# Scratch matrix products around the group-norm chains of a four-layer block

## The chip, the cores and the metric

One core of one Trainium2 chip runs the whole program. The metric is the device time of one execution in microseconds (us). A kernel is executed several times and the median is given; beside it stands one execution that the hardware profiler recorded.

## The reference, cut to what matters

The input is one image of 256 x 256 positions with 128 channels, in 32-bit floats. Four layers follow each other, and each adds its result to its own input after a group norm over the whole image:

```python
def _gn(v, G=32, eps=1e-5):
    g = v.reshape(B_, H_, W_, G, C_ // G)
    m = jnp.mean(g, axis=(1, 2, 4), keepdims=True)
    s = jnp.var(g, axis=(1, 2, 4), keepdims=True)
    return ((g - m) / jnp.sqrt(s + eps)).reshape(v.shape)

x = x + _L0_conv_ref(_gn(x), ...)   # attention along the rows, 4 heads
x = x + _L1_conv_ref(_gn(x), ...)   # a gated recurrence of 16 steps
x = x + _L2_conv_ref(_gn(x), ...)   # products over pairs of rows, gated
x = x + _L3_conv_ref(_gn(x), ...)   # a 3x3 convolution and a 128x128 matrix
```

A group is 4 neighbouring channels over all positions. So no layer can apply its norm before the last element of the layer in front of it is there: the mean and the variance of the whole image stand between any two layers.

## The kernel before, in words

Channels lie on the 128 partitions, positions along the free dimension. Each layer streams the image from DRAM in blocks, computes, writes its sum back to DRAM and gathers statistics as it goes. The four stages are the methods `attention`, `recurrence`, `triangle` and `convolution`; `run` (L1475) calls them in that order.

**The group norm between stages.** `group_affine` (L75) turns the statistics of 128 channels into a scale and an offset for each channel, the two columns of the tile `ab`. It is a chain of tiny steps that wait for each other:

1. VectorE makes mean and variance of each channel, `mv` (L99 to L120; in the first stage they come from `statistics`).
2. TensorE averages the means over a group: `pm`, a product with the 128x128 matrix `g4` and one moving column (L81).
3. VectorE copies it to `mg`, and forms the group's variance terms `gd` and `gv` (L83 to L87).
4. TensorE averages those: `pv` (L89).
5. ScalarE takes the root, `sd` (L91); VectorE makes `ab` from it (L93, L94).

Every product goes through the helper `mm` (L59, its line in the profile is L60). In float32 one product is recorded as two TensorE instructions, "passes" below, and two weight loads. `group_affine` is called four times:

- L352, in `attention`, after `statistics`. After it come `centering` (L129: the tile `lc` and the product `pc`), and then the block loop: transposes `pt` (L394), their copies `xo` (L395), the centring products `zc` (L403), their copies `zs` (L405), and so on.
- L845, in `recurrence`. After it come the products `pab` (L852) and `rpbf`, `rpbi`, `rpbd` (L860) with `ab`, and the block loop, whose first products are the gate `zd` (L912), then `za`, `m`, `zf`.
- L1075, in `triangle`. After it come `centering`, a product `tpbo` (L1081) and the block loop with `zc` (L1137), `zs` (L1139).
- L1365, in `convolution`. After it the taps `U` get a term (L1369), a bias tile `bw` is made through the product `cpbw` (L1374, L1375), ScalarE normalises rows into `xp` (L1394), VectorE transforms them into `v` (L1411 to L1426), and TensorE multiplies `v` with `U` into `m` (L1436): 24 x 3 products of 128x128 for each half block of 8 rows, 32 half blocks. VectorE and ScalarE turn `m` into output rows (L1444 to L1458), POOL issues their store (L1460).

**What sets the order.** A scheduler arranges the instructions of each engine by its own estimate of their times, except those that were given to `keep_in_program_order` (`pin`), which stay in the order of the code. Each engine works its list in order and waits there on semaphores. Tiles come from pools: a new tile takes the place of an older one, and its first writer waits for the last reader of the old one. PSUM pools are opened and closed around each stage, so the small pools around `group_affine` (`awq` L351, `rwp` L844, `twp` L1074, `cxp` L1364) take banks that the stage before has just used.

Of the kernel before, what the change touches and what calls it, by code (L numbers as in the profile page):

```python
# [9 lines left out]
F32 = mybir.dt.float32  # L10
# [7 lines left out]
P = 128  # L18
# [12 lines left out]
class Kernel:  # L31
# [27 lines left out]
    def mm(self, out, lhsT, rhs, start=True, stop=True):  # L59
        return self.nc.tensor.matmul(out, lhsT, rhs, start=start, stop=stop)  # L60

    def column(self, pool, src, name):

        t = pool.tile([src.shape[0], 1], F32, name=name)
        self.nc.sync.dma_start(t, src.rearrange("(c o) -> c o", o=1))
        return t
# [5 lines left out]

    def group_affine(self, pool, psum, stats, group, tag, whole=False, shift=None, mv=None):  # L75

        nc = self.nc
        if mv is None:
            mv = self.mean_variance(pool, stats, tag, shift)
        pm = psum.tile([P, 2], F32, name=f"pm{tag}", tag="gn")  # L80
        self.mm(pm[:, 0:1], group, mv[:, 0:1])  # L81
        mg = pool.tile([P, 1], F32, name=f"mg{tag}")
        nc.vector.tensor_copy(mg, pm[:, 0:1])  # L83
        d = pool.tile([P, 1], F32, name=f"gd{tag}")
        nc.vector.tensor_sub(d, mv[:, 0:1], mg)
        v = pool.tile([P, 1], F32, name=f"gv{tag}")
        nc.vector.scalar_tensor_tensor(v, d, d, mv[:, 1:2], ALU.mult, ALU.add)  # L87
        pv = psum.tile([P, 2], F32, name=f"pv{tag}", tag="gn")
        self.mm(pv[:, 0:1], group, v)  # L89
        sd = pool.tile([P, 1], F32, name=f"sd{tag}")  # L90
        self.chain("table", self.act(sd, pv[:, 0:1], AF.Sqrt, bias=self.eps))  # L91
        ab = pool.tile([P, 2], F32, name=f"ab{tag}")
        nc.vector.reciprocal(ab[:, 0:1], sd)  # L93
        nc.vector.scalar_tensor_tensor(ab[:, 1:2], mg, -1.0, ab[:, 0:1], ALU.mult, ALU.mult)  # L94
        if whole:
            return ab, mg, sd
        return ab
# [961 lines left out]
    def triangle(self, x2T, x3T, znT, prodD, stats2, shift2, stats3, prepare):  # L1059
# [6 lines left out]
        pin = lambda f: lambda *a, **k: tc.keep_in_program_order(f(*a, **k))  # L1066
# [5 lines left out]
        with ExitStack() as c:  # L1072
            wp = c.enter_context(self.pool(name="tw", bufs=1))
            with self.pool(name="twp", bufs=2, space=PSUM) as ps0:  # L1074
                ab = self.group_affine(wp, ps0, stats2, self.g4, "2", shift=shift2)  # L1075
                lc, cb = self.centering(wp, ps0, ab, "2")
                W = self.weights
                lnw, lnb, low, lob = (W[n] for n in ("in_w", "in_b", "out_w", "out_b"))
                wpg, oraw, we = W, W["o"], W["e"]
                pb = ps0.tile([P, 2], F32, name="tpbo", tag="gn")  # L1080
                self.mm(pb[:, 0:1], oraw, lob)  # L1081
                wbo = wp.tile([P, 1], F32, name="twbo")
                V.tensor_copy(wbo, pb[:, 0:1])
                wo = wp.tile([P, P], F32, name="two")
                V.tensor_scalar_mul(wo, oraw, low)

                wf = wp.tile([P, G, 4, CQ], F32, name="wf")
                for n, m in enumerate("gp"):
                    for side in range(2):
                        V.tensor_copy(wf[:, :, 2 * n + side, :],  # L1090
                                      wpg[m][:, side * P:(side + 1) * P].rearrange("c (g d) -> c g d", g=G))
# [240 lines left out]
    def convolution(self, x3T, stats3, late):  # L1332
# [27 lines left out]
        with ExitStack() as c:  # L1360
            wp = c.enter_context(self.pool(name="cx", bufs=1))
            bw = wp.tile([P, P], F32, name="bw")
            with ExitStack() as c0:
                ps0 = c0.enter_context(self.pool(name="cxp", bufs=2, space=PSUM))  # L1364
                ab, mg, sd = self.group_affine(wp, ps0, stats3, self.g4, "3", True)  # L1365
                dg = wp.tile([P, P], F32, name="dg3")
                V.tensor_scalar_mul(dg, self.ident, sd)
                for n, f in ((1, -1.0 / 6), (2, 1.0 / 6), (3, 1.0 / 12), (4, -1.0 / 12)):
                    V.scalar_tensor_tensor(U[:, n, 1, :], dg, f, U[:, n, 1, :], MUL, ADD)  # L1369

                bc = wp.tile([P, P], F32, name="bc")
                V.tensor_scalar(bc, bwc.to_broadcast([P, P]), mg, 0.0, ADD, ADD)
                pbw = ps0.tile([P, P], F32, name="cpbw")
                self.mm(pbw, bc, self.ident)  # L1374
                V.tensor_copy(bw, pbw)  # L1375
            io = c.enter_context(self.pool(name="c1", bufs=2))
            tp = c.enter_context(self.pool(name="c2", bufs=1))
            yp = c.enter_context(self.pool(name="c3", bufs=2))
            pm = c.enter_context(self.pool(name="c1m", bufs=8, space=PSUM))
# [194 lines left out]
```

## Time and profile before

| what | value |
|---|---|
| median of 3 executions | 5099.39 us (5096.98 to 5099.84) |
| the profiled execution | 5096.92 us |
| its span, first to last instruction | 5095.1 us |
| time around the span | 1.8 us |
| TensorE busy | 4938.7 us, 97% of the span |
| VectorE busy | 4100.7 us, 80% |
| ScalarE busy | 3497.2 us, 69% |
| mean granted TensorE clock | 0.990 |

Starts of the four `pm` products in the span: 128.63, 1694.91, 3225.62 and 4560.35 us. So the stages are, roughly: statistics up to 129 us, attention to 1695 us, recurrence to 3226 us, triangle to 4560 us, convolution to the end.

In the profile, PE is TensorE (its products), PEld its weight loads, DVE VectorE, ACT ScalarE, POOL GpSimd. A row of the timeline gives start, length, engine, line and operation, tiles (out<-in), shapes, the count of instructions merged into it, and in brackets how long the engine sat idle before it and what ended that. A row of the windows gives the busy time of each engine in one stretch of the span, the clock that TensorE was granted in it as a share of the full one (PEclk), the busy share of the DMA engines and their rate. A PE row's busy time counts the latency of the pipeline too, so it overstates how much the array streams.

### The profile page before, as it was taken

To read this page: it belongs to the slowest core of one execution; us is meant where nothing else is said; L and a number is where in the kernel's file an instruction comes from. 1 tells how busy PE (TensorE), PEld (TensorE's weight loads), DVE (VectorE), ACT (ScalarE), POOL (GpSimd) and SP (SyncE) were. 2 spreads that over 40 slices of the span, in tenths; PEclk is the share of its full clock that TensorE was granted. 3 is DMA by queue.
4 is the path that set the end of the run, shared out by engine and by line. 5 is a ranking of instruction groups with operands and counts; after the bars stand their busy time and mean duration, and the time that the engine had idled before them with its cause. 6 is when DMAs were issued, how large, how long until landed. Compare 5 with 4: busy or idle time off the path is not lost. (4 is left out here: it accounts for less than half of the span.)

```text
span 5095.1 us, 78580 instructions
## 1 busy us (share of the span) xinstructions
PE 4938.7 (97%) x31357; PEld 2699.4 (53%) x31357; DVE 4100.7 (80%) x4797; ACT 3497.2 (69%) x4948; POOL 406.9 (8%) x592
## 2 busy tenths in 40 slices
PE   8999999999999899999999999899999999989999
PEld 2444555555555333333333333229999953349999
DVE  6666999999999799999999999775333537779886
ACT  6445888888888899999999999453333357762110
POOL 0331000000000000000000000240111010000000
PEclk9999999999999899999999999999999999999999
DMA  8894222222222222222222221588666778865432
GB/s 289 291 338 173 88 84 80 88 81 82 84 81 82 65 70 66 74 64 76 64 74 66 72 68 61 215 324 308 235 230 243 252 286 321 322 230 181 141 122 67
DMA packets 204461, 781.66 MB, mean 153 GB/s; under 512 B 56278, under 2 KB 59628, under 8 KB 154788
## 3 DMA queue, kind: packets, MB, share of 16 engines
q1 hardware_dynamic: 146638, 505.57, 29.6%
q0 software_dynamic: 56160, 270.64, 14.7%
q8 instruction: 250, 4.10, 0.3%
q14 instruction: 117, 0.96, 0.1%
q10 hardware_dynamic: 1296, 0.40, 0.0%
HBM read 505.18 MB, written 271.32 MB: 152 GB/s over the span
## 5 line engine op out<-in xcount | busy, mean ns | idle before, releaser
L565 DVE TENSOR_TENSOR e<-sc,bT 128x1024 f32<-128x1024 f32 x512 | 603.1, 1220 | 51.3 <-PE sc L60 50.4
L54 ACT ACTIVATE e<-e 128x1024 f32<-128x1024 f32 x512 | 540.3, 1055 | 63.1 <-DVE e L565 53.9
L1066 DVE TENSOR_TENSOR LR<-z,sg 128x512 f32<-128x512 f32 x256 | 268.6, 1049 | 363.5 <-ACT sg L54 363.5
L60 PE MATMUL m<-U,v 128*128 128x128 f32 x4608 | 516.9, 276 | 6.7 <-DVE v L1413 6.7
L60 PEld LDWEIGHTS m<-U,v 128*128 128x128 f32 x4608 | 516.8, 193 | 6.7 <-DVE v L1413 6.7
L60 PEld LDWEIGHTS z<-wf,zt 128*128 128x128 f32 x4096 | 460.0, 193 | 2.9 <-DVE zn L1066 2.7
L60 PE MATMUL z<-wf,zt 128*128 128x128 f32 x4096 | 460.2, 276 | 1.3 <-DVE zn L1066 1.3
L54 ACT ACTIVATE sg<-z 128x512 f32<-128x512 f32 x256 | 153.0, 597 | 308.8 <-PE z L60 308.8
L54 ACT ACTIVATE sq<-zs 128x1024 f32<-128x1024 f32 x192 | 202.4, 1054 | 196.3 <-DVE zs L374 156.9
L565 DVE TENSOR_TENSOR ks<-e 128x1024 f32<-128x1024 f32 x256 | 300.9, 1217 | 0.0
L60 PE MATMUL sc<-tq,tk 32*128 32x256 f32 x4096 | 297.7, 402 | 3.2 <-DVE e L565 2.3
L60 PEld LDWEIGHTS sc<-tq,tk 32*128 32x128 f32 x4096 | 186.9, 185 | 160.5 <-issue 97.1
L60 PE MATMUL nd<-e,tv 128*32 128x256 f32 x4096 | 271.7, 383 | 0.0
L54 ACT ACTIVATE dn<-dn 128x512 f32<-128x512 f32 x384 | 241.7, 629 | 14.2 <-DVE dn L565 3.4
L60 PE MATMUL av<-y,ident 128*128 128x512 f32 x384 | 191.3, 607 | 44.8 <-DVE y L903 44.8
L60 PE MATMUL po<-LR 128*128 128x256 f32 x1024 | 222.2, 380 | 7.0 <-DVE LR L1066 7.0
L1450 ACT COPY m4s<-m 128x512 f32<-128x512 f32 x32 | 18.7, 585 | 286.1 <-PE m L60 286.1
L60 PEld LDWEIGHTS po<-LR 128*128 128x128 f32 x1024 | 194.1, 190 | 34.2 <-DVE LR L1066 7.7
L60 PE MATMUL bx<-p,ident 128*128 128x512 f32 x384 | 193.3, 612 | 0.0
L54 ACT ACTIVATE o<-po 128x256 f32<-128x256 f32 x256 | 84.3, 381 | 145.3 <-issue 109.4
L60 PEld LDWEIGHTS nd<-e,tv 128*32 128x32 f32 x4096 | 120.2, 110 | 108.9 <-issue 42.9
L54 ACT ACTIVATE xp<-xr,ab 128x1536 f32<-128x1536 f32 (+1 forms) x48 | 76.9, 1653 | 137.6 <-DVE tf L1425 126.7
(364 smaller groups left out, 10354.7 us busy)
## 6 DMA issues: line engine op xcount, KB each, us to landing
zt<-znT SPq DMA_DIRECT2D x128, 1024.0 KB
znT<-zn POOLq DMA_DIRECT2D x64, 1024.0 KB, 5.2
xin<-x2T SPq DMA_DIRECT2D x64, 1024.0 KB
xin<-in_x_dram SPq DMA_DIRECT2D x50, 1024.0 KB
xr<-x3T SPq DMA_DIRECT2D x46, 768.0 KB
xT<-xo POOLq DMA_DIRECT2D x32, 1024.0 KB, 9.4
xr<-xT SPq DMA_DIRECT2D x64, 512.0 KB
zn<-znT SPq DMA_DIRECT2D x64, 512.0 KB
```

The lines of the kernel that those rows point to most:

```text
L54: return self.nc.scalar.activation(out, in_, func, bias=bias, scale=scale, **kw)
L60: return self.nc.tensor.matmul(out, lhsT, rhs, start=start, stop=stop)
L565: pin = lambda f: lambda *a, **k: tc.keep_in_program_order(f(*a, **k))
L1066: pin = lambda f: lambda *a, **k: tc.keep_in_program_order(f(*a, **k))
L1450: nc.scalar.copy(m4, m[4])
```

## The change: what it does

A helper `keep_busy` issues `n` products of the identity matrix with the matrix `cmat` into a PSUM scratch tile `busy` that nothing reads. Both operands are 128x128 and lie in SBUF from the start. `group_affine` calls it three times: before `pm` (8 products; 11 in `triangle`, 26 in `convolution`), after `pm` (3) and after `pv` (3). `convolution` calls it once more after `cpbw` (26). `pm`, `pv` and the new products are pinned.

```diff
+    def keep_busy(self, psum, n):
+        t = psum.tile([P, P], F32, name="busy", tag="busy", bufs=1)
+        for _ in range(n):
+            self.tc.keep_in_program_order(self.mm(t, self.ident, self.cmat))
...
-    def group_affine(self, pool, psum, stats, group, tag, whole=False, shift=None, mv=None):
+    def group_affine(self, pool, psum, stats, group, tag, whole=False, shift=None, mv=None, busy=8):
...
+        pin = self.tc.keep_in_program_order
         pm = psum.tile([P, 2], F32, name=f"pm{tag}", tag="gn")
-        self.mm(pm[:, 0:1], group, mv[:, 0:1])
+        self.keep_busy(psum, busy)
+        pin(self.mm(pm[:, 0:1], group, mv[:, 0:1]))
+        self.keep_busy(psum, 3)
...
-        self.mm(pv[:, 0:1], group, v)
+        pin(self.mm(pv[:, 0:1], group, v))
+        self.keep_busy(psum, 3)
...
-                ab = self.group_affine(wp, ps0, stats2, self.g4, "2", shift=shift2)
+                ab = self.group_affine(wp, ps0, stats2, self.g4, "2", shift=shift2, busy=11)
...
-                ab, mg, sd = self.group_affine(wp, ps0, stats3, self.g4, "3", True)
+                ab, mg, sd = self.group_affine(wp, ps0, stats3, self.g4, "3", True, busy=26)
...
                 self.mm(pbw, bc, self.ident)
                 V.tensor_copy(bw, pbw)
+                self.keep_busy(ps0, 26)
```

In the built program this gives TensorE 14, 14, 17 and 58 products more at the four places. The order of the others changes in few spots: in `convolution` `pv` now stands before `cpbw`, and the three products after `pv` stand after `cpbw` together with the 26, so that 29 stand in a row before the first `m`. On VectorE, the step L119 of `recurrence` and L111 of `convolution` move ahead of the copy `mg`, and in the first four blocks of `convolution` some transform steps (`te`, `tf`, `v`, `ta`) change places with the row steps `r`, `s`, `ys`; ScalarE and POOL swap a few `xp` steps and stores there. Nothing is added on any engine but TensorE.

## The prediction, made before the result was known

> **What bounds the kernel now.** I read the page first: busy shares, the clock row, the costliest groups.
>
> ```profile
> PE   8999999999999899999999999899999999989999
> ...
> PEclk9999999999999899999999999999999999999999
> ...
> L60 PE MATMUL m<-U,v 128*128 128x128 f32 x4608 | 516.9, 276 | 6.7 <-DVE v L1413 6.7
> ```
>
> TensorE leads nearly everywhere, and in the convolution it sets the end alone: 4608 passes, idle 6.7 us in all, and that before the first. The mean clock, 0.990, hides where the clock is low, so I cut the span into windows around the four norms and moved the edges until each window had one clock. Around the last norm:
>
> ```profile
> 4553.22:4556.61 3.39, 0.15 (x1) 0.00 (x0) 3.36 (x4) 0.00 (x0) 0.00 (x0) 1.00 0.00 0
> 4556.63:4560.02 3.39, 0.00 (x0) 0.00 (x0) 3.28 (x5) 0.00 (x0) 1.10 (x6) 0.50 0.19 77
> 4560.04:4563.43 3.39, 1.57 (x6) 1.43 (x6) 1.90 (x13) 0.30 (x2) 0.00 (x0) 0.50 0.57 232
> 4563.46:4566.85 3.39, 0.00 (x0) 0.00 (x0) 1.61 (x6) 3.39 (x3) 0.00 (x0) 0.50 0.00 0
> 4566.87:4570.26 3.39, 1.04 (x5) 1.04 (x6) 3.39 (x6) 1.10 (x1) 0.00 (x0) 0.50 0.33 67
> 4570.29:4573.68 3.39, 3.39 (x18) 3.39 (x18) 3.39 (x7) 1.42 (x1) 0.00 (x0) 0.50 1.02 428
> 4573.70:4577.10 3.40, 3.40 (x32) 3.40 (x32) 3.40 (x7) 1.91 (x2) 0.00 (x0) 1.00 0.51 205
> ```
>
> PE's busy time is the second number, the clock the third from the end. An idle window is followed by half clock, a full one by full clock (18 passes in 3.39 us, then 32). The other norms look alike: half clock at 129.5 to 136.4, 1692.8 to 1703.1 and 3225.4 to 3235.7. The timeline shows what ran then:
>
> ```profile
> 128.63 0.35 PE L60 MATMUL pm<-mvx,g 128*128 128x1 f32 x2 [0.80 <-DVE mvx L268]
> ...
> 131.90 3.65 PE L374 MATMUL pt<-ident,kept 128*128 128x128 f32 x16 [0.30 <-issue]
> ...
> 139.29 1.91 PE L374 MATMUL pt<-ident,kept 128*128 128x128 f32 x16
> ...
> 1694.91 0.59 PE L60 MATMUL pm<-mv,g 128*128 128x1 f32 x2 [2.42 <-DVE mv L115]
> ...
> 1699.82 3.54 PE L60 MATMUL zd<-xf,gwd 128*64 128x512 f32 x8 [0.26 <-DVE gbd L862]
> ...
> 3229.59 8.42 PE L60 MATMUL zc<-xin,lc 128*128 128x512 f32 x12 [0.25 <-DVE twbo L1083]
> ...
> 4569.22 35.99 PE L60 MATMUL m<-U,v 128*128 128x128 f32 x301 [6.66 <-DVE v L1413]
> ```
>
> The same sixteen transposes take 3.65 us at half clock and 1.91 at full; a chain product 0.59 and 0.35. So after each norm the next stage starts slow.
>
> **What the Trainium skill says.** TensorE: Matmul & The Clock Gate, Part 1, has the clock at half after an idle window of about 3.4 us and at full after a busy one, the window free-running. The trace agrees: every change lies on one grid of 3.413 us. It does not say how busy is busy. Counting a pass as its columns / 1.2 ns at full clock and twice that at half, windows of this trace that lowered the clock streamed at most 0.42 of their length (two with 0.37 and 0.40 did not lower it); those that left it low at most 0.75, those that raised it at least 0.88. Part 2, step by step, has products in program order, only weight loads overtaking: whatever stands before `pm` delays it. FP8 and Floating Point Precision, TensorE Precision Notes, has four array passes for a float32 product; agreed: 1131 recorded passes of `m` in the 126.0 us from 4574 on are 0.1114 us each, two records a product, 0.223 us, near 4 x 128 columns at 2.4 GHz (0.213). That is my price of a scratch product, same shape and type: 0.223 at full clock, 0.446 at half.
>
> **The change part by part.** The waits are from the built order. Times are the profiled execution's (5096.92 us, span 5095.10).
>
> First norm. The 8 products follow `pmx`, whose last pass leaves the array at about 127.8, and end at 127.8 + 1.8 = 129.6; `pm` could go at 128.6, so it is 0.9 late. The next window still streams about 0.6 (six products 1.3 us, transposes 0.7, of 3.41), so the clock stays full. `pv` and `pc` gain 0.24 each, so the transposes start at 131.90 + 0.9 - 0.5 = 132.3. Eight of them and the 1.0 us copy on ScalarE put `zc` at 134.5 instead of 135.34, and a further 1.0 us of `zc` until 136.36 loses its half: 0.8 + 0.5, near 1.4 us.
>
> Second. The products wait for VectorE's `og` and the product before, both done; they follow the last output product, free at 1691.37 + 0.86 = 1692.2, and end at 1694.0, before `pm` at 1694.9. A program branch lies between; I take it at nothing (VectorE's own shows none: `negid` starts at 1693.14 while its last step ends), bound 0 to 2 us; at 1 us the window to 1692.8 stays idle, products run at half clock and `pm` is up to 1.5 us late. Else: `pm`, `pv` 0.5, L119 ahead of `mg` 0.1, sixteen small bias products and their copies 2.17 to 1.5 (estimate), `zd` 3.54 to 1.88 as later ones take: 2.9 us. What is late next is ScalarE (busy 3.04 of 3.39 us from 1703.1), which starts with `zd`, so the shift stays.
>
> Third. The 11 products wait for ScalarE's `ig`, long done, follow `po` at 3222.4 and end at 3224.9, before `pm` at 3225.6: free. `pm`, `pv` gain 0.24 each, `pc` and `tpbo` 0.24 each. Of `zc`, eight passes reach VectorE's second `zs` at 3236.33, 6.7 us after their start; at full clock 8 x 0.427 + 0.3 = 3.7. Sum 1.0 + 3.0, 3.9 us with rounding.
>
> Fourth. The 26 wait for VectorE's `gate(0)` (to 4553.04) and the last `py` (4553.2), and end at 4559.1; `pm` at 4560.3 does not feel them. `pm` and `pv`, now ahead of `cpbw`, bring `xp` and with it `m` to 4568.65, 0.6 early (`bw` before the reciprocal takes 0.2 of it back). The 29 start near 4562.0 and end at 4568.5: they just fit; past that they delay `m`. `m` runs at full clock, instead of 4.47 us at half: 2.2 us. Sum 2.8.
>
> The moved VectorE, ScalarE and POOL steps of the first convolution blocks cost nothing: a block takes VectorE about 13.2 (22 row steps of 0.60) + 13.7 (12 transform steps of 1.14) = 27 us, beside 144 products x 0.223 = 32.1. Without this slack, about one step, 1.2 us. No DMA is moved.
>
> Do the shifts reach the end? The block loop before the attention stores a block of `xT` every 9.5 us from 151.9 to 428.7, and triangle's first loop one of `znT` every 6.3; TensorE is busy 20.0 of 20 us in the one and over 18.6 of 20 in the other, with DMA under its limit at first (0.58 from 180 to 200 us). Such even loops shift as a whole.
>
> Sum at this execution's grid: 1.4 + 2.9 + 3.9 + 2.8 = 11.0. But the grid is free: I moved its edge through 3.41 us in 40 steps with the thresholds above; the sums are 7.0 to 11.3, mean 9.6 (1.3, 2.4, 3.0, 2.9). From the median of 5099.39, itself over many grids, 9.6 off gives 5089.8: **5090 us**. The profiled execution lies 2.5 us under that median; 5096.92 - 11.0 = 5085.9 would be its own.
>
> **The rivals.**
> - The six products inside a chain don't hold the clock: their 1.34 us are 0.39 of a window, at the limit of 0.37 to 0.42. Then transposes, `zd` and `zc` lose 1.5 to 1.7 us each: 9.6 - 4.9 = 4.7, 5094.7. For it: the margin; against: small products and the next stage's first ones add to the window. 0.18.
> - The starts of the first three stages are hidden (by DMA, or ScalarE in the recurrence), only the convolution gains: 5096.5. Against: the even periods. 0.08.
> - More than counted: the half clock of the recurrence's first loops (1706.5 to 1713.3, 1730.4 to 1737.2) goes as well: 5085. Against: ScalarE is full there. 0.06.
> - Slower: products of an identity don't count as activity (the change doesn't do what it says). The clock falls as before, and those after the fall cost 0.446: first `pm` 0.9 late, second 0.7, fourth 1.2; the 29, from about 4563, take 12.9 us to 4576, where `m` could go at 4569.9: 6.1; seven groups of three 0.4 each: 2.8. Sum 11.7, 5111. It decides from about 0.37 us a product, where lateness eats the gain. Against: `m` raises the clock with passes of this shape. 0.06.
>
> **How the numbers follow.** Forecast 0.62, rivals as given. A measurement of this kernel can tell about 0.2%, 10.2 us, from no change; the forecast's 9.6 sits just inside, with about 0.42 of it beyond. Faster: 0.62 x 0.42 + 0.06 = 0.32; slower 0.06; the rest 0.62. The range 5085 to 5097 takes in the forecast's 7 to 11.3, the branch, the first rival and most of the second; the slower one and the tails, under 0.2, stay out.
>
> **What would show it.** Right: full clock in all windows from 126 to 140, 1693 to 1703, 3222 to 3239 and 4553 to 4577; sixteen `pt` in 1.9 us; `zd` in 1.9; first `zc` twelve in about 5.3; `m` from its start 32 passes a window; `pm` on time but for the first. Wrong: half clock in any of these, a last scratch product after `v` is ready, or an early stage start that is gone by the stage's end.

## The result, and the profile after

| | before | with the change |
|---|---|---|
| median of 13 executions each | 5098.49 us (5093.95 to 5099.96) | 5087.26 us (5084.85 to 5090.56) |
| ratio, 95% interval | | 0.998 (0.9973 to 0.9987) |
| span of the profiled execution | 5095.1 us | 5083.0 us |
| mean granted TensorE clock | 0.990 | 0.995 |

The change is faster by 11.2 us, 0.2%; the interval of the ratio, times 5098.49, is 6.6 to 13.8 us. Forecast were 5090 us and a gain of 9.6. Two slow executions of the kernel before (5619 and 11236 us) are left out of the medians below.

The page first: the row of the clock, and the products of the convolution, which no longer wait at all.

```profile
PEclk9999999999999999999999999999999999999999
...
L60 PE MATMUL m<-U,v 128*128 128x128 f32 x4608 | 514.8, 275 | 0.0
```

The one dip in the clock row of before is gone, but the row still hides 44 us of half clock: its slices are 127 us long, a window 3.4. So the windows again, laid on the changed kernel's own clock grid, around the fourth norm (busy time of PE, PEld, DVE, ACT and POOL, then the clock):

```profile
4549.88:4553.28 3.40, 2.44 (x18) 2.16 (x18) 2.36 (x13) 0.26 (x1) 0.06 (x1) 1.00 0.77 313
4553.30:4556.69 3.39, 3.33 (x30) 3.29 (x30) 1.60 (x7) 3.28 (x3) 0.00 (x0) 1.00 0.00 0
4556.71:4560.10 3.39, 3.39 (x32) 3.39 (x32) 3.39 (x6) 1.28 (x1) 0.00 (x0) 1.00 0.29 56
```

Before, this stretch had 17 us of half clock; now it has none, and the window in which `m` starts (4559.31) takes its 32 passes like every later one. The weakest window, the first one shown, holds `pm`, three products, `pv`, `cpbw` and the first of the 29: 18 passes, not all with 128 columns. It streams 0.47 of its length (no pass is counted under 25 ns; by columns alone it is 0.44), and windows that streamed up to 0.42 have lowered the clock in the profile of before. The timeline at the four norms (lines of the changed kernel lie 7 to 12 further down; `pt` is L385 for L374 in the profile of before):

```profile
127.67 2.03 PE L60 MATMUL busy<-cmat,ident 128*128 128x128 f32 x16
129.54 0.28 PE L60 MATMUL pm<-mvx,g 128*128 128x1 f32 x2
...
132.32 1.94 PE L385 MATMUL pt<-ident,kept 128*128 128x128 f32 x16 [0.30 <-issue]
134.49 3.70 PE L60 MATMUL zc<-xo,lc 128*128 128x512 f32 x8 [0.23 <-ACT xo L385]
...
1690.28 3.21 PE L60 MATMUL busy<-cmat,ident 128*128 128x128 f32 x16
1693.33 0.28 PE L60 MATMUL pm<-mv,g 128*128 128x1 f32 x2
...
1697.03 1.94 PE L60 MATMUL zd<-xf,gwd 128*64 128x512 f32 x8 [0.26 <-DVE gbd L873]
...
3221.05 0.38 PE L60 MATMUL pm<-mv,g 128*128 128x1 f32 x2 [0.45 <-DVE mv L126]
...
3224.20 5.42 PE L60 MATMUL zc<-xin,lc 128*128 128x512 f32 x12 [0.25 <-DVE twbo L1094]
...
4552.51 6.96 PE L60 MATMUL busy<-cmat,ident 128*128 128x128 f32 x58
4559.31 20.86 PE L60 MATMUL m<-U,v 128*128 128x128 f32 x185
```

Sixteen `pt` in 1.94 us for 3.65, eight `zd` in 1.94 for 3.54, the first twelve `zc` in 5.42 for 8.42. `pm` of the first norm follows its scratch products with no idle time: it is 0.9 us late, as forecast. `m` follows its 29 products in the same way, 0.81 us after the first `v` starts, where before it was 0.74: there is no slack left.

To tell the places apart I measure a stretch around each norm that begins before the scratch products act and ends where the next stage runs evenly: from the copy `accs` to the first `var`; from `negid` to the first `m` of the recurrence; from VectorE's last step that `pm` needs (`mv`, L115 of before) to the first `pr`; from the start of the last eight `py` passes to the third copy `m4s` of the convolution. Each is read from one profile (us):

| kernel | first | second | third | fourth |
|---|---|---|---|---|
| before | 15.10 | 14.87 | 16.25 | 64.89 |
| the change | 13.86 | 12.47 | 12.44 | 62.30 |
| gain | 1.24 | 2.40 | 3.81 | 2.59 |

Together 10.0 us. Stretches without scratch products (the kernel before, and e1 and e3 below) agree within 0.2 us at the first, second and fourth norm, but lie between 14.79 and 16.25 at the third: of its 3.8 us, up to 1.5 may be the grid's. The two profiled executions lie 12.1 us apart; the other 2.0 came and went between the norms, where nothing was edited. There the clock falls at other places too, and whether it does depends on how the grid lies. The end of the block loop in front of the attention lost 1.5 us in the changed kernel's profile, since this window lowered its clock (0.37 of it streamed), where the like one of before (0.43) had not:

```profile
440.20:443.60 3.40, 1.59 (x10) 0.29 (x8) 2.30 (x3) 0.00 (x0) 2.43 (x3) 1.00 0.01 3
443.70:447.00 3.30, 3.30 (x7) 1.09 (x4) 0.78 (x2) 0.01 (x1) 0.42 (x1) 0.50 0.78 319
```

In the same way the end of the attention (near 1680) gave 2.2 us, the filling of the recurrence 1.4 and the middle of triangle (3437) 1.1, and the end of the recurrence (3205) took 1.2.

### The profile page after: what moved, and what is told of

It is laid out like the page before. It is cut to its first block, busy times and chain, and to the rows that moved or that the text cites. A ratio compares the mean times of both kernels' runs of the same rounds, so it can differ in the third digit from the quotient of the medians.

```text
span 5083.0 us, 78992 instructions
## 1 busy us (share of the span) xinstructions
PE 4951.9 (97%) x31563; PEld 2715.8 (53%) x31563; DVE 4100.4 (81%) x4797; ACT 3496.8 (69%) x4948; POOL 406.9 (8%) x592
## 4 chain that ended last, share of the span: by engine, by line
PE 57%; DVE 29%; issue 5%; ACT 1%; POOL 0%; DMA 0%; POOLq 0%; DVEq 0%; SPq 0%; ACTq 0%
PE z L60 9%; PE m L60 7%; PE nd L60 7%; PE sc L60 5%; PE zc L60 5%; PE po L60 4%; DVE tr L917 3%; DVE t L914 3%; DVE y L914 3%; DVE p L914 3%; DVE yf L914 3%; PE ppq L60 3%; PE ppv L60 2%; PE px L60 2%; PE pe L60 2%
```

## The experiments

All edits are to the changed kernel unless stated. Every median stands beside the kernel before on the same chip; the stretches are read from one profile each. The ratios of e1, e2, e3 and e5 have 1 in their interval: as whole times these are not told apart from the kernel before, and what they show is in the stretches and the clock. Here are all stretches, for looking up:

| run | first | second | third | fourth | median | before | ratio (95%) |
|---|---|---|---|---|---|---|---|
| e1 order only | 15.05 | 14.95 | 16.14 | 64.83 | 5098.01 | 5096.76 | 1.0002 (0.9993 to 1.0010) |
| e2 leading only | 15.03 | 16.35 | 14.13 | 62.15 | 5095.32 | 5096.76 | 0.9998 (0.9990 to 1.0007) |
| e3 convolution only | 15.11 | 15.03 | 14.79 | 62.30 | 5094.69 | 5096.76 | 0.9993 (0.9985 to 1.0002) |
| e4 one column | 17.69 | 15.20 | 16.60 | 71.77 | 5106.18 | 5096.76 | 1.0019 (1.0011 to 1.0027) |
| e5 half | 14.81 | 15.95 | 14.13 | 62.76 | 5095.08 | 5099.03 | 0.9993 (0.9985 to 1.0002) |
| e6 double | 16.76 | 15.38 | 15.21 | 73.64 | 5106.63 | 5099.03 | 1.0017 (1.0010 to 1.0024) |
| e7 more places | 13.86 | 12.09 | 12.43 | 62.29 | 5082.93 | 5099.03 | 0.9969 (0.9957 to 0.9981) |
| e8 places that pay | 13.86 | 12.86 | 12.44 | 62.30 | 5078.28 | 5096.48 | 0.9967 (0.9955 to 0.9979) |
| e9 change again | 13.86 | 12.10 | 12.44 | 63.79 | 5085.97 | 5096.48 | 0.9980 (0.9973 to 0.9988) |

### Is it the products, or the order they bring?

```diff
     def keep_busy(self, psum, n):
+        return
```

> The order and the pins of the change without one scratch product. My theory (the gain is the clock that stays full): the half clock at the four norms is back, the sixteen pt take about 3.65 us, the eight zd about 3.5, the first twelve zc about 8.4, m starts with 18 passes a window; the only gain is that pv no longer waits behind cpbw, 0 to 0.6 us, so 5098 (5095 to 5100). Rival (the rearranged order brings the gain): 5087, and m starts 2 us or more earlier against its pm than the 8.9 us of before.

Measured 5098.01 us, no gain, and half clock at all four norms:

```profile
132.28 3.65 PE L385 MATMUL pt<-ident,kept 128*128 128x128 f32 x16 [0.30 <-issue]
...
4566.21 14.06 PE L60 MATMUL m<-U,v 128*128 128x128 f32 x105 [6.66 <-DVE v L1425]
```

The pins alone do nothing. They do not even bring `pv` ahead of `cpbw`: without the products the scheduler keeps the order of before there, so the expected 0 to 0.6 us is 0, and this run says nothing of that order. The next one does: it has `cpbw` ahead of `pv` as well, and still wins 2.7 us at the fourth norm. There `m` starts 8.26 us after `pm`, with the change 8.47, before 8.87. So the order isn't what brings the gain.

### Do the small groups inside the chain matter?

```diff
-        self.keep_busy(psum, 3)
...
-        self.keep_busy(psum, 3)
```

> The products in front of pm and the 26 ahead of m stay, the groups of three after pm and after pv are gone. My theory (a window must stream more than about 0.45 of its length, so a break between two products matters as well as the wait in front of pm): the clock falls one window later in the first three stage starts; locally 0.5 us gained at the first, 0.7 at the second, 0.7 at the third, 2.5 at the fourth, 4.4 in all, 5094 (5091 to 5097). Rival (the threes are ornament, the leading groups hold the clock): full clock as in the whole change, pm 0.4 us earlier after each pause, 5087 or less.

Measured 5095.32 us, and the gains are 0.1, -1.5, 2.1 and 2.7 us. The first three starts are slow again: `pt` 3.53 us, `zd` 3.38, `zc` 7.11. So the threes do hold the clock, and at the fourth norm, where the 26 ahead of `m` follow soon, they are not needed: without them the stretch is even 0.15 us shorter. The second norm lost more than expected, and not through the clock alone:

```profile
1696.09 3.57 PE L60 MATMUL busy<-cmat,ident 128*128 128x128 f32 x16 [1.83 <-DVE negid L853]
1699.50 0.28 PE L60 MATMUL pm<-mv,g 128*128 128x1 f32 x2
```

TensorE stood still for 1.83 us between the last `px` and the scratch products, although these wait for nothing that was late; then they ran at half clock, in 0.43 us each, and `pm` was 2.8 us late. The same kernel once more:

> The kernel with only the leading groups once more, for one look at the second norm: there TensorE stood still for 1.83 us between the last output product and the scratch products, which the change itself does not show. If the program's layout causes that standstill, it is there again, at 1.8 us, and pm is 2 us or more late; if it is chance, pm is late by less than 1 us. The windows at the other norms as before: pt 3.5 us, zc 7 to 8.4 us, m at full clock.

```profile
1695.90 3.75 PE L60 MATMUL busy<-cmat,ident 128*128 128x128 f32 x16 [2.49 <-DVE me L128]
1699.45 0.42 PE L60 MATMUL pm<-mv,g 128*128 128x1 f32 x2
```

It is there again, 2.49 us long, and `pm` again over 3 us late (one execution, 5095.58 us). At the first norm the grid lay better than expected: `pt` took 2.74 us, not 3.5. The kernel with half the products shows one of 1.69 us, and the last version below one of 1.34 us in the middle of the scratch group, where nothing can be waited for:

```profile
1686.68 0.94 PE L60 MATMUL busy<-cmat,ident 128*128 128x128 f32 x7
1688.96 1.27 PE L60 MATMUL busy<-cmat,ident 128*128 128x128 f32 x9 [1.34 <-issue]
```

The change in its two profiles shows none, nor do the ones with one column, with twice the products and with more places. So it belongs to the program's layout. The place is behind the end of a program branch. The Trainium skill (Runtime: NRT & Kernel Launch, Instruction fetch mechanics) says that a taken branch to a page which is not loaded waits for its fetch. The records fit. Queue 8 brings one block of 16 KB for about 257 recorded instructions of TensorE (250 blocks in the kernel before), so I take it for TensorE's own program. One such block is loaded at this branch in every profile. In the five without a standstill the block in front of it had come only 28 to 168 instructions earlier; in the four with one, it was 184, 238, 270 and 274 instructions earlier, and the standstills are 1.34, 1.69, 1.83 and 2.49 us, in the same order. In these four TensorE goes on 2.2 to 2.7 us after the load at the branch starts. The kernel before, e1 and e3 have no product that could run there. No run moved the branch, so the cause is likely and not proved.

### Does each place count by itself?

```diff
-    def group_affine(self, pool, psum, stats, group, tag, ..., busy=8):
+    def group_affine(self, pool, psum, stats, group, tag, ..., busy=0):
...
-        self.keep_busy(psum, 3)
+        self.keep_busy(psum, 3 if busy else 0)
...
-                ab = self.group_affine(..., busy=11)
+                ab = self.group_affine(..., busy=0)
```

> Scratch products only at the fourth norm (26, 3, 3 and 26). My theory (each stage start gives its own gain and all reach the end): the fourth alone, 2.6 us against the kernel before, 5095.9 (5093 to 5098). Rival (starts of the first three stages are hidden, the convolution carries the change): 5087.

Measured 5094.69 us; the fourth stretch is 62.30, exactly that of the whole change. The rival, 5087, is out (the interval ends at 5089): the first three norms carry most of the gain. The third stretch shows how much a grid can do alone: 14.79 us for 16.25 with nothing added, since here the clock was low for two windows, and before for three.

### What counts as activity?

```diff
-            self.tc.keep_in_program_order(self.mm(t, self.ident, self.cmat))
+            self.tc.keep_in_program_order(self.mm(t[:, 0:1], self.ident, self.cmat[:, 0:1]))
```

> The same number of scratch products in the same places, each with one moving column instead of 128, so TensorE has as many instructions and weight loads but streams next to nothing. My theory (what counts is how much of a window the array streams): the clock falls at all four norms as without them, sixteen pt 3.65 us, zc 8.4, m 18 passes a window at first; 5098 (5095 to 5100). Rival (any instruction or weight load that keeps the queue from idling counts): full clock at least where the groups are long, in front of the fourth pm and of m, and 5091 or less.

The clock fell at all four norms, as expected, but the time was 5106.18 us, 9 us over the kernel before, not the same. I had taken one-column products to be short. They are not. First the windows, then the timeline at the fourth norm:

```profile
4551.87:4555.26 3.39, 3.39 (x31) 3.15 (x29) 3.32 (x5) 0.00 (x0) 0.00 (x0) 1.00 0.00 0
4555.28:4558.67 3.39, 3.39 (x19) 3.39 (x18) 3.29 (x5) 0.00 (x0) 1.10 (x6) 0.50 0.09 39
4558.69:4562.08 3.39, 3.39 (x18) 3.39 (x18) 1.40 (x9) 0.00 (x0) 0.00 (x0) 0.50 0.66 271
```

```profile
4562.93 12.73 PE L60 MATMUL busy<-cmat,ident 128*128 128x1 f32 x58
4575.53 4.65 PE L60 MATMUL m<-U,v 128*128 128x128 f32 x24
```

Both TensorE columns of the first window are as full as they can be, 31 passes and 29 weight loads, and still the clock is halved after it. So neither instructions nor weight loads count, but what streams through the array. And a pass with one column takes as long as one with 128: in either group, each pass with its weight load, the passes start 0.11 us apart at full clock. At half clock 29 products take 12.73 us, 0.44 each, and hold `m` back by 5.8 us: `v` starts at 4568.99, and before `m` followed its start by 0.74. This is what the slower rival of the prediction described: scratch products that do not hold the clock cost twice their price and sit in the way. It was priced at 11.7 us over the kernel before; here it is 9.4.

### How many are enough, and how many too many?

```diff
-        self.keep_busy(psum, 3)
+        self.keep_busy(psum, 1)
...
-                self.keep_busy(ps0, 26)
+                self.keep_busy(ps0, 13)
```

So far e5, in which the default of `busy` is 4 for 8, and 6 and 13 stand for 11 and 26; e6 has 6 for 3, 52 for 26, and 16, 22 and 52 for `busy`.

> Half the scratch products: 4, 4, 6 and 13 in front of pm, one after pm and one after pv, 13 ahead of m. My theory (a window of 3.413 us must stream more than about 0.45 of its length): 4 products are 0.25 of a window, 13 leave 4 us idle behind them, so the clock falls at all four norms, and the gain is gone but for what a lucky grid leaves: 0.3, 0.3, 0.8 and 0.5 us locally, 5096 (5092 to 5099). Rival (any break shorter than a window is enough): full clock at least at the first three norms, pm on time at the first, 5088 or less.

Measured 5095.08 us, not told apart from the kernel before. The clock falls at all four norms, `pt` 3.65 us, `zd` 3.68, `zc` 7.11. The gains are 0.3, -1.1, 2.1 and 2.1: at the second norm `pm` is late again behind the standstill, and at the last two it did better than I had said, 2.1 for 0.8 and 0.5; of the third's, 1.5 may be the grid's. At the fourth the 14 products in front of `m` made the clock rise at 4562.0, ahead of `m`:

```profile
4549.14 3.06 PE L60 MATMUL busy<-cmat,ident 128*128 128x128 f32 x26
4556.28 0.56 PE L60 MATMUL pm<-mv,g 128*128 128x1 f32 x2 [4.08 <-DVE md L120]
```

The break of 4.08 us behind the 13 leading products is what lowered it.

> Twice the scratch products: 16, 16, 22 and 52 in front of pm, six after pm and after pv, 52 ahead of m. My theory (a product costs nothing while something else is waited for, and 0.223 to 0.24 us each once the waiting is used up): full clock, but against the whole change 3.0 us later at the first norm, 1.9 at the second, 2.9 at the third, 11.0 at the fourth (4.4 at pm, 1.2 in the chain, the rest ahead of m), 18.8 in all: 5106 (5102 to 5110). Rival (TensorE has nothing else to do there, more of them can do no harm): 5087.

```profile
128.71 3.82 PE L60 MATMUL busy<-cmat,ident 128*128 128x128 f32 x32
132.36 0.28 PE L60 MATMUL pm<-mvx,g 128*128 128x1 f32 x2
...
1695.27 4.81 PE L60 MATMUL busy<-cmat,ident 128*128 128x128 f32 x32
...
4554.61 11.77 PE L60 MATMUL busy<-cmat,ident 128*128 128x128 f32 x104
4566.22 0.28 PE L60 MATMUL pm<-mv,g 128*128 128x1 f32 x2
```

Measured 5106.63 us for 5106. Against the change the stretches are 2.9, 2.9, 2.8 and 11.3 us longer (expected 3.0, 1.9, 2.9 and 11.0). The clock is full at three norms. At the second it is half from 1694.1 to 1697.5, since the end of the attention had let it fall; the 16 products there take 4.81 us, 1.0 more than at the first norm, and that is the 1.0 us missed. The price of a product once the waiting is used up is 0.24 us at the first norm (3.82 / 16) and 0.226 in the longer group of the fourth (11.77 / 52).

### Half clock elsewhere

The helper gets a tag, so that its tile takes a place among the tiles that a loop has anyway:

```diff
+            self.keep_busy(ps, 5, (P, 1024), "w", 3)
             pair_bias(NM - 1)
...
+            self.keep_busy(ps, 7, (P, 512), "pj", 2)
             output(rp)
...
+            fills = {(0, "m2"): 12, (1, "za"): 6, (1, "zi"): 8, (NB, "pa"): 10, (NB + 1, "av"): 26}
...
+                        n = fills.get((it, step.__name__), 0)
+                        if n:
+                            self.keep_busy(ps, n, (P, 512), "s", 2)
                         step(D[it - lag])
...
+                    if m == NB // 2 - 1:
+                        self.keep_busy(ps, 5, (P, 512), "r", 2)
                     pr = spreads(ps, rs)
```

> The whole change and scratch products in the other waits that are followed by half clock: 5 + 5 + 5 in the last block of the loop in front of the attention, 8 and 7 ahead of the last two px, 12, 6 and 8 in the first two steps of the recurrence (ahead of m2, za, zi) and 10 and 26 in its last two (ahead of pa and av), 5 + 5 at the end of triangle's first loop. My theory (the clock costs time wherever TensorE's products follow on the path): 1.0 at the first, 1.2 at the second, 1.5 in the filling and 2.5 in the draining of the recurrence, 1.2 in triangle, some 7 us under the whole change, 5080 (5077 to 5084). Rival (there ScalarE and VectorE set the pace, and the half clock is hidden): 5087, with the clock full and the following steps no earlier.

Measured 5082.93 us. From 100 us on, before the last few, the profile has 17 us of half clock, where the kernel before has 89 and the change 44. Against their kernels before, this run wins 16.1 us and the change 11.2, so the new places give 4.9 us where 7 were expected. Not every place paid. At the end of triangle's first loop the clock was held and the products of `z` came 2.5 us earlier against what went ahead, only to wait for a transfer:

```profile
3426.83 10.98 PE L60 MATMUL z<-wf,zt 128*128 128x128 f32 x96
3440.40 34.85 PE L60 MATMUL z<-wf,zt 128*128 128x128 f32 x310 [2.59 <-DMA zt<-znT]
```

There the rival was right: what is late next is a load of `zt`. The filling of the recurrence gave 2.2 us against before, where the change's profile has 1.4 without an edit; that ScalarE sets most of the pace there is argued from its first `m`, which waits for ScalarE's `a` in both, and not tested. So the last version leaves triangle alone and adds products where that run still had half clock (the edit against that run):

```diff
             for i in range(2):
+                self.keep_busy(ps, 2 + i, (P, 512), "pj", 2)
                 score(i)
...
+                if rp == 0:
+                    self.keep_busy(ps, 3, (P, 512), "pj", 2)
                 score(a + 2)
...
-                    if m == NB // 2 - 1:
-                        self.keep_busy(ps, 5, (P, 512), "r", 2)
```

> The run with more places, without the 5 + 5 products at the end of triangle's first loop (there the products of z came 2.5 us earlier and then waited 2.6 us for a transfer), and with 2, 3 and 3 more ahead of the first three scores of the attention, where that run still had 10.2 us of half clock. My theory (half clock costs only where nothing else is late next): the attention starts 1.0 us earlier than in that run, triangle loses nothing, 5082 (5079 to 5085), and some 5 us under the change itself on the same chip. Rival (VectorE's e sets the pace of the first scores, and the end of triangle's loop was worth its 1.1 us on most grids): 5083 to 5085.

Measured 5078.28 us, the fastest: 18 us under the kernel before, 7.7 under the change on the same chip (expected 5). The score groups run at full clock, and two stretches of half clock are left after 100 us, 10.2 us in all. At the first scores this run gains 2.2 us on the kernel before, where the run with more places lost 0.9; 1.0 between the two was expected, it is 3.1. Here `z` runs through without that wait:

```profile
3423.73 56.50 PE L60 MATMUL z<-wf,zt 128*128 128x128 f32 x489 [1.37 <-DVE zn L1092]
```

### The change once more, on another grid

> The change itself once more, unaltered, beside the run of the places that pay and with another position of the clock's grid. My theory: the four places give 10 us again (1.2, 2.4, 3.8 and 2.6 us), what lies between them moves by the luck of the grid by up to 2 us either way, 5087 (5085 to 5090). Rival (part of the gain at the four places was luck of one grid): a place gives 1 us or more less than in the first profile.

Measured 5085.97 us. The first three places gave 1.24, 2.77 and 3.81 us again, but the fourth only 1.10, so the rival is right for that one:

```profile
4549.49:4552.88 3.39, 2.21 (x18) 1.86 (x17) 2.74 (x11) 0.00 (x0) 1.03 (x6) 1.00 0.75 309
4552.90:4556.29 3.39, 3.33 (x16) 3.04 (x16) 1.81 (x9) 2.35 (x3) 0.00 (x0) 0.50 0.02 5
```

```profile
4553.25 8.32 PE L60 MATMUL busy<-cmat,ident 128*128 128x128 f32 x58
4561.41 10.77 PE L60 MATMUL m<-U,v 128*128 128x128 f32 x95
```

The same work as in the change's first profile, but the grid cuts it elsewhere: this window streams 0.41 of its length, not 0.47. The clock falls for one window, the 29 products take 8.32 us, not 6.96, and `m` starts 1.5 us later after `pm`.

## Why the prediction held, step by step

- **The mechanism** is shown: no products, no gain (e1); the same number without streaming, a loss (e4); the old order with the clock held, the same gain at the fourth norm (e2).
- **First norm**, forecast 1.4 on this grid: 1.24. `pm` 0.9 us late (measured 0.91), the transposes at 132.3 (132.32), `zc` at 134.5 (134.49).
- **Second**, forecast 2.9: 2.40, and 2.77 in e9. The products follow `px` at once, so the branch cost nothing, as taken; but in the first profile the clock was already low from 1689.5 on, eight products took 3.05 us, and `pm` was 0.4 us late (it starts 0.71 us after the start of `mv`, before 0.29). The 0 us taken for the branch came true by the luck of the layout: others show standstills of 1.3 to 2.5 us, past the bound of 2.
- **Third**, forecast 3.9: 3.81 twice, against one profile of before whose grid was unkind: e3 had 1.46 of it with no products.
- **Fourth**, forecast 2.8: 2.59, and 1.10 in e9. "They just fit; past that they delay m" was the weak point of the sum, and what pushes them past it is their own clock. The 0.6 us put down to `pv` ahead of `cpbw` is a misreading: with the old order (e2) `m` came 0.61 us earlier after `pm`, with the new one 0.40. And at half clock a product took 0.43 us (its passes start 0.213 apart), not 0.446.
- **The sum**, 11.0 on the traced grid and 9.6 in the mean: 10.0 and 8.9 at the places, in two profiles. Measured as a whole 11.2 (6.6 to 13.8) and, in e9, 10.5. That the whole lies above the sum of the places is luck: 2.0 us of the first profile and 1.1 of the second arose where nothing was edited.
- **Rivals.** That six products in a chain do not hold the clock is out as a rule: in two profiles they held it at seven of eight norms, with 0.47 streamed at the weakest. At the fourth of e9, with 0.41, they did not: the margin was as thin as feared. That the first three starts are hidden is out (e3). That the recurrence's filling gains as well is not settled by the medians; in the profile it shifted by 1.4 us, with its clock's stretches placed otherwise. The slower rival exists (e4), not in this change. Even block loops pass a shift on, as said: the first norm's 1.25 us stand unchanged from 139 to 443 us, the second's through the recurrence. What I did not foresee is how such a shift dies: not in the loop but at its end, where the grid decides anew.

## What to carry to other kernels

Where TensorE bounds both sides of a small chain of waits, look at its clock in windows, not in the page's slices; if it halves there, scratch products with many columns, put into the waits, win part of the slow stretch (here 10.0 of the 44.6 us of half clock at the four norms), so long as they end before what waits behind them. Count by the share of a window that streams and by time, not by instructions, and leave some slack at both ends, since the grid is not yours: the fourth place lost 1.5 us by 0.06 of a window. Then ask at each place what is late next; where it is a transfer, as at the end of triangle's first loop, the clock is not worth holding.

## What the runs showed of the hardware

- Over all twelve profiles, from 100 us on, windows with less than 0.35 streamed lowered the clock every time (68 of 68), those with 0.35 to 0.55 sometimes (35 of 177), those above never. A low clock rose in 1 of 27 windows with 0.60 to 0.75, in 102 of 108 above 0.75, and never below 0.60. Streaming is counted as in the prediction, from columns, with no pass under 25 ns; the limits were chosen with these windows in sight and carry the error of the count. The Trainium skill (TensorE: Matmul & The Clock Gate, Part 1) has an idle window lower the clock and a busy one raise it; idle is wider than empty.
- Float32 passes with one moving column started 0.11 us apart at full clock and 0.21 at half, the same as those with 128.
- TensorE stood still for 1.3 to 2.5 us behind a branch in four profiles and not in five; the four were those in which its block of instructions ahead of the branch had been loaded longest ago, 184 instructions or more.
